# A two-layer graph network on one core: four small moves in a fixed instruction order (sums in the projection, byte casts in the attention, a fetch of rows, sums of the last product)

## The chip, the cores and the metric

The kernel runs on one core of one Trainium2 chip. The metric is the device time of one execution in microseconds (us). The kernel before was timed three times: 2682.81, 2682.03 and 2674.33 us, so its median is 2682.03 us. A profile of one more execution gives, for every instruction, when it ran and what it waited for.

## The reference, cut to what matters

```python
# x [3327, 512], adj [3327, 3327] (0 or 1, about 1% ones), W_stack [2, 512, 1024], weight [512, 512]; all float32
def gat(x, W, adj):
    Wh, Ws = split(x @ W, 2, axis=-1)
    a = softmax(Wh @ Ws.T, axis=-1) * adj
    return leaky_relu(a @ Wh + x, 0.01)

y = x
for l in range(2):
    y = gat(y, W_stack[l], adj)
x = layernorm(x + y)

bw = sign(weight)
ba = maximum(sign(x), 0)
out = relu(adj @ (ba @ bw.T))
return layernorm(x + out)
```

There are three kinds of large products: the projections and scores of each of the two attention layers, the attention's weighted sums `a @ Wh`, and at the end the aggregation `adj @ (...)` with a 0/1 matrix.

## The kernel before, in words

**Blocks and sums.** Rows are cut into 26 tiles of 128 (`P`). Two tiles are a pair (13 pairs, `NQ`), four tiles a chunk (7 chunks, `NC`). Nearly every large product is computed as a 2 x 2 block product with seven multiplications in place of eight. That needs sums of the left blocks (`left_sums`, L180 to L183) and of the right blocks (`right_sums`, L186 to L189) on VectorE, and copies (ScalarE) and additions (VectorE) that put the seven products together in PSUM and out of it (`seven`, L144 to L173; copies named p1, p5, u2, u3). In PSUM the lane `ch` has three banks, `acc` four, `tr` one.

**A fixed order.** No scheduler chooses the order of instructions. The Python code writes it out, and every engine (TensorE, VectorE, ScalarE, GpSimd as POOL, and SyncE, which only issues transfers) runs its own instructions strictly in the order in which they were written. Two helpers make the order. In the projection `weave` (L191) takes several lists of small steps and merges them, so that step i of a list of n lies at (i + 0.5)/n of the way. In the attention each step gathers pairs of a key and an action and runs them sorted by key (L911); a key of 0.6 means about 60% of the way through the step. Small blocks in SBUF come from one ring of 33 slots (`slot`), which are reused in order.

**The projection** (`project`, L243 to L449, once for each layer) computes for each chunk c, from the transposed rows `xT`:
- the "chains" `one` and `two` (`queries`): a product with the matrix `m`. They need the sums `xt` of the chunk (`sums`, four right sums made by `prepare(c)`), and give blocks `gsp`. At their end `done` (L400) stores three blocks, forms the four right sums of the results, and stores them also, all in `gs_d`.
- the "pairs" (`project_values(c, a)`, two for a chunk): first `keys` (L310), which makes the four left sums of the keys in tiles `s12` and `s34` and issues six stores to `xs_d` from POOL (L324 to L327), then seven products with the weights (L338), whose results stay in `wh`, and at the end `done` (L343), four right sums in tiles `t12` and `t34` with two stores to `ws_d`.
- the "turns": four transposes of the next chunk's rows (L263), and `prepare(c + 1)`.

The loop of L435 to L449 weaves these three lists for each chunk. The pairs of a chunk are created when its turn in the loop comes, so the first pair's `keys` opens the chunk, and both `done` steps close it.

**The attention** (`attention`, L463 to L933, once for each layer) runs 169 steps, 13 row halves g times 13 pairs q. The scores (L494) run 30 steps ahead of the values (L719). Between them lie, for one block of scores: the subtraction of the maximum (`shift`, L639, VectorE), the exponential (L642, ScalarE), a running sum (L650, VectorE), the mask by the adjacency block (`masked`, L655, VectorE), and four sums on POOL (L692 to L695, tile `as`). SyncE loads `ws`, `adj`, `xs` and, once for a chunk, `gs` (1792 KB).

**Byte blocks.** Since adj holds only 0 and 1, each block is also kept for the last product as seven small blocks in fp8, in a tile `ab` (tag `adj_b`, two buffers). `halved` (L658) casts three blocks on ScalarE (L663, L664). `halved_sums` (L666) makes four sums on VectorE (L674), `exact` (L679) checks on VectorE that the block is 0/1 (and takes adj's name out of the table), and `keep_blocks` (L676) issues the 112 KB store to `adj_d` from POOL. Each of the 169 blocks is kept once, about half of them in each layer. In the step's list the four have these keys, the last one in the following step:

```python
(-0.1, lambda: halved(*of)), (0.6, lambda: halved_sums(*of)),
(0.62, lambda: exact(*of)),
...
after.append((0.05, lambda of=of: keep_blocks(*of)))
```

**The end of a row half** (`finish`, L755 to L836) divides by the sum of the exponentials and adds the rows of x (`residual`), and in the second layer also takes the sign (`sign`, tile `ba`), transposes it (`turn`, tile `pbt`) and multiplies it by `bw` (`linear`). The rows come by `fetch(i)`: one load of 256 KB (`xres`) for the row tile in the first layer, two (`xres` and `x0`) in the second. `fetch(0)` is called twice in succession (L827, L828).

**The last product.** While the attention's last row half runs, `load_products` loads the rows `xw` and makes the right sums of the first 11 (`EARLY`) of 13 pairs (`product_sums`, in the tiles `wh`). After the last step the nine actions of the last `finish` run, with part of the last product between them (`fill`, L926). Then `finale` makes the product sums of the pairs 11 and 12 (L1074, L1075) and runs the rest of the aggregation (`aggregate`, L992).

Of the kernel before, what the change touches and what calls it, by code (L numbers as in the profile page):

```python
# [11 lines left out]
F8 = mybir.dt.float8e4  # L12
# [7 lines left out]
P = 128  # L20
# [9 lines left out]
def kernel(  # L30
# [15 lines left out]
    NQ = NT // 2  # L46
# [5 lines left out]
    def tiles_of(c):  # L52
        return range(c * CT, min(NT, (c + 1) * CT))
# [137 lines left out]
    def weave(*lists):  # L191

        at = [
            ((i + 0.5) / len(part), n, do)
            for n, part in enumerate(lists) for i, do in enumerate(part)
        ]
        for _, _, do in sorted(at, key=lambda e: e[:2]):
            do()
# [44 lines left out]
    def project(l, pre):  # L243
# [172 lines left out]
                for e in range(2):  # L416
                    nc.scalar.copy(m[:, 2 * e : 2 * e + 2], m_of[l][e])

        chains = {}

        def prepare(c):
            start, *chains[c] = queries(c, (ch_lane, ch_lane if c else acc_lane))
            if start:
                start()
# [10 lines left out]
        for c in range(NC):  # L435
            turns = []
            if c + 1 < NC:
                turns = [lambda k=k: transpose_x(c + 1, k, tr_lane) for k in range(KD)]
                turns.append(lambda: prepare(c + 1))
            if c + 2 < NC:  # L440
                load_x(c + 2)
            if c == 0:
                weave(*chains[c], turns)
            else:
                one, two = chains[c]
                pairs = []
                for a in range(len(tiles_of(c)) // 2):
                    pairs += project_values(c, a, acc_lane)
                weave(one + two, pairs, turns)  # L449

    bw = []

# [10 lines left out]
    def attention(l, att):  # L463
# [193 lines left out]

        def halved(g, q):  # L658

            at = adj[g, q]  # L660
            t = att.tile([P, 7, P], F8, tag="adj_b", bufs=2, name=f"ab_{g}_{q}")
            adj[g, q, "b"] = t
            nc.scalar.copy(t[:, 0:2], at[:, :, :P], saturate=False)  # L663
            nc.scalar.copy(t[:, 2], at[:, 1, P:], saturate=False)  # L664

        def halved_sums(g, q):  # L666
            at, t = adj[g, q], adj[g, q, "b"]
            a11, a21, a12, a22 = (at[:, k, ts(i, P)] for k in range(2) for i in range(2))
            s1, s2, s3, s4 = (t[:, i] for i in range(3, 7))
            for to, a, b, op in (  # L670
                (s1, a21, a22, ALU.add), (s2, s1, a11, ALU.subtract),
                (s3, a11, a21, ALU.subtract), (s4, a12, s2, ALU.subtract),
            ):
                nc.vector.tensor_tensor(to, a, b, op, saturate=False)  # L674

        def keep_blocks(g, q):  # L676
            nc.gpsimd.dma_start(out=adj_d[g][:, q], in_=adj.pop((g, q, "b")))

        def exact(g, q):  # L679

            at = adj.pop((g, q))
            i = g * NQ + q
            nc.vector.scalar_tensor_tensor(
                at, at, 0.0, at, ALU.is_gt, ALU.not_equal, accum_out=cnt[:, i : i + 1],
            )
# [69 lines left out]
        def finish(g):  # L755

            sm = total[g][:, 0]
            nc.gpsimd.tensor_tensor(sm, sm, total[g][:, 1], ALU.add)
            pz = ps_tr.tile([P, 2, P], F32, tag="tr", name=f"pz_{l}_{g}")
            rz = small.tile([P, 2], F32, tag="rz", name=f"rz_{l}_{g}")  # L760
            hs = out_.pop(g)
            mine = half_tiles(g)
            held = {}

            def norm():
                for i in range(2):
                    nc.tensor.transpose(pz[:, i], sm[:, ts(i, P)], ident)
                nc.vector.reduce_sum(rz, pz, axis=AX.X)
                nc.vector.reciprocal(rz, rz)

            def fetch(i):
                t = mine[i]
                span = slice(t * P, t * P + rows(t))
                for name, src in (("xres", x1_d), ("x0", x)) if last else (("xres", x),):
                    xr = ring.tile([P, D], F32, tag="xr", name=f"{name}_{l}_{t}")
                    load_rows(nc.sync, xr, src[span, :], rows(t))
                    held[i, name] = xr

            def residual(i):
                t, hh = mine[i], hs[i]  # L780
                r = rows(t)
                span = slice(t * P, t * P + r)
                nc.vector.scalar_tensor_tensor(
                    hh[:r], hh[:r], rz[:r, i : i + 1], held[i, "xres"][:r], ALU.mult, ALU.add
                )
                nc.vector.scalar_tensor_tensor(
                    hh[:r], hh[:r], NEG_SLOPE, hh[:r], ALU.mult, ALU.max
                )
                if last:
                    nc.vector.tensor_tensor(hh[:r], hh[:r], held[i, "x0"][:r], ALU.add)  # L790
                load_rows(nc.gpsimd, h_d[span, :] if last else x1_d[span, :], hh, r)

            def sign(i):

                t, hh = mine[i], hs[i]
                r = rows(t)
                st = small.tile([P, 6], F32, tag="bn", name=f"bn_{t}")
                nc.vector.bn_stats(st[:r], hh[:r])
                nc.vector.bn_aggr(mv[:r, t, :], st[:r])
                ba = held[i] = att.tile([P, D], BF16, tag="ba", bufs=1, name=f"ba_{t}")  # L800
                nc.vector.tensor_scalar(ba[:r], hh[:r], mv[:r, t, 0:1], None, ALU.is_gt)

            def turn(i):
                r = rows(mine[i])
                pt = ps_tr.tile([P, KD, P], BF16, tag="tr", name=f"pbt_{mine[i]}")
                for k in range(KD):
                    nc.tensor.transpose(pt[:, k, :r], held[i][:r, ts(k, P)], ident_h[:r, :r])
                held[i] = att.tile([P, KD, P], BF16, tag="baT", bufs=1, name=f"baT_{mine[i]}")
                nc.scalar.copy(held[i][:, :, :r], pt[:, :, :r])

            def linear(i):

                t = mine[i]
                r = rows(t)
                pw = ps_tr.tile([P, D], F32, tag="tr", name=f"pxw_{t}")
                for k in range(KD):
                    nc.tensor.matmul(
                        pw[:r], held[i][:, k, :r], bw[k], start=(k == 0), stop=(k == KD - 1)
                    )
                if g == NQ - 1:  # L820
                    nc.scalar.copy(xw[t][:r], pw[:r])
                    return
                xh = att.tile([P, D], F16, tag="ba", bufs=1, name=f"xwh_{t}")
                nc.scalar.copy(xh[:r], pw[:r])
                load_rows(nc.gpsimd, xw_d[t], xh, r)

            fetch(0)  # L827
            fetch(0)  # L828
            if not last:
                return [norm, lambda: residual(0), lambda: fetch(1), lambda: None,  # L830
                        lambda: residual(1)]
            return [
                norm, lambda: residual(0), lambda: (sign(0), fetch(1)), lambda: turn(0),
                lambda: linear(0), lambda: residual(1), lambda: sign(1), lambda: turn(1),
                lambda: linear(1),
            ]  # L836
# [3 lines left out]
        else:  # L840
# [17 lines left out]
            n = len(steps) - end - 2  # L858
# [15 lines left out]
        later, after = [], []  # L874
        for v in range(-LOOK - 4, len(steps)):
# [17 lines left out]
            if 0 <= v + 2 < len(steps):  # L893
                s2 = steps[v + 2]
                work += [(0.01, lambda: running(*s2)), (0.4, lambda: masked(*s2))]
                of = blocks.get(v + 2)
                if of:
                    work += [
                        (-0.1, lambda: halved(*of)), (0.6, lambda: halved_sums(*of)),
                        (0.62, lambda: exact(*of)),  # L900
                    ]
                    after.append((0.05, lambda of=of: keep_blocks(*of)))
            if later:
                work += [(0.7, later.pop(0))]
            if 0 <= u < len(ahead):
# [17 lines left out]
            (g, b, p, i) for g in range(2) for b in range(3) for p in range(EARLY)  # L923
            for i in BANKS[b]
        ]
        for n, do in zip((4, 16, 48, 8, 12, 12, 12, 8, 8), later):  # L926
            do()
            for e in fill[:n]:
                aggregate(*e)
            fill = fill[n:]  # L930
# [40 lines left out]
    def product_sums(p):  # L971
        x1, x2 = xw[2 * p], xw[2 * p + 1]
        xt[p] = wh[p].bitcast(F16).rearrange("p a n -> p (a n)")[:, : 4 * HD].rearrange(
            "p (i n) -> p i n", i=4
        )
        right_sums(x1[:, :HD], x1[:, HD:], x2[:, :HD], x2[:, HD:], *(xt[p][:, i] for i in range(4)))
# [20 lines left out]
    def finale(att):  # L997
# [73 lines left out]
            nc.vector.tensor_copy(flag_i, flag)  # L1071

        constants()
        for p in range(EARLY, NQ):  # L1074
            product_sums(p)  # L1075
        load_h(0)
        for g in range(NQ):
            todo = [
# [103 lines left out]
```

## Time and profile before

| What | Value |
|---|---|
| times of three runs | 2682.81, 2682.03, 2674.33 us (median 2682.03) |
| the profiled execution's own time | 2681.87 us |
| its span in the profile | 2680.1 us |
| granted TensorE clock, mean | 0.996 |
| TensorE matmuls, busy | 2622.6 us, 98% of the span |
| TensorE weight loads, busy (beside the matmuls) | 2273.6 us, 85% |
| VectorE, busy | 2059.8 us, 77% |
| ScalarE, busy | 813.0 us, 30% |
| POOL, busy | 1093.4 us, 41% |
| DMA | 648.84 MB, 242 GB/s in the mean |

The span reaches from the first to the last recorded instruction; the execution's own time lies 1.8 us above it. A line of a timeline or a group names the line of the code, the engine, the operation, and then the tile that is written and those that are read ("s<-xT"). "x4" is the number of instructions in succession that are put together. In square brackets stands the idle time of the engine just before the line, in us, and what ended it. A row of the waits has the waiting engine, tile and line, what it waited for, and then three numbers: the sum in us, how many times, and the longest. A row of the windows has the stretch, its length, the busy time (and number of instructions) of TensorE, its weight loads, VectorE, ScalarE and POOL, the granted clock, the share of the DMA engines and their GB/s.

### The profile page before, as it was taken

The page shows a single profiled execution, that of the slowest core. Times are in us where ns is not written, and L with a number is a line of the kernel's source. Part 1 is how long each engine was busy: PE and PEld are TensorE (multiplying, and loading weights), DVE is VectorE, ACT ScalarE, POOL GpSimd, SP SyncE. Part 2 cuts the span into 40 slices and gives each one's busy share as a digit, 9 for nine tenths or more (in the row PEclk, how much of TensorE's full clock was granted, in tenths as well). Part 3 has the DMA queues.
Part 4 walks back from the last instruction along what each step waited for, and adds up shares of the span by engine and source line. Part 5 has one row for each costly group of instructions (what it writes and reads, how often), then busy time and mean ns, then how long its engine had stood idle before and what let it go on. Part 6 is the DMA issues. An engine that isn't in the chain of part 4 may idle for free. (4 is left out here: it accounts for less than half of the span.)

```text
span 2680.1 us, 40370 instructions
## 1 busy us (share of the span) xinstructions
PE 2622.6 (98%) x12839; PEld 2273.6 (85%) x12864; DVE 2059.8 (77%) x4211; ACT 813.0 (30%) x2000; POOL 1093.4 (41%) x2029
## 2 busy tenths in 40 slices
PE   9999999999999999999999999999999999999897
PEld 7888888888888888887888888888888888888787
DVE  5554888899888996666755488988899888767876
ACT  3333332333323332221332333333333333222142
POOL 2450343444434444546543044444444444455510
PEclk9999999999999999999999999999999999999999
DMA  5754777777777776777865578777777777787874
GB/s 197 259 199 151 253 253 238 241 278 249 256 234 251 276 243 235 232 252 237 292 207 180 196 230 285 252 248 268 245 273 253 260 265 230 236 269 268 285 247 159
DMA packets 290800, 648.84 MB, mean 242 GB/s; under 512 B 32765, under 2 KB 147295, under 8 KB 289046
## 3 DMA queue, kind: packets, MB, share of 16 engines
q1 hardware_dynamic: 254822, 539.75, 60.8%
q0 software_dynamic: 35760, 106.45, 10.9%
q8 instruction: 105, 1.72, 0.2%
q14 instruction: 113, 0.93, 0.1%
HBM read 539.13 MB, written 106.93 MB: 241 GB/s over the span
## 5 line engine op out<-in xcount | busy, mean ns | idle before, releaser
L494 PE MATMUL pZ<-gs,xs 128*128 128x256 f32 x2496 | 640.3, 381 | 10.9 <-ACT u L511 9.7
L692 POOL TENSOR_TENSOR as<-s 128x128 f32<-128x128 f32 x338 | 163.9, 485 | 1011.1 <-DVE s L655 661.3
L494 PEld LDWEIGHTS pZ<-gs,xs 128*128 128x128 f32 x2496 | 475.1, 191 | 79.6 <-ACT u L511 12.8
L719 PE MATMUL acc<-ws,s 128*128 128x256 f32 x1352 | 403.1, 380 | 0.0
L719 PE MATMUL acc<-wh,s 128*128 128x256 f32 x1352 | 356.1, 380 | 0.0
L719 PE MATMUL acc<-ws,as 128*128 128x256 f32 x1352 | 349.9, 380 | 5.5 <-DMA ws<-ws_d 4.6
L494 PE MATMUL pY<-gs,xs 128*128 128x256 f32 x1248 | 320.3, 379 | 0.0
L642 ACT ACTIVATE s<-s 128x512 f32<-128x512 f32 x338 | 213.4, 631 | 317.3 <-DVE s L639 316.8
L719 PEld LDWEIGHTS acc<-ws,as 128*128 128x128 f32 x1352 | 254.8, 190 | 46.7 <-issue 5.1
L719 PEld LDWEIGHTS acc<-wh,s 128*128 128x128 f32 x1352 | 257.6, 191 | 35.4
L719 PEld LDWEIGHTS acc<-ws,s 128*128 128x128 f32 x1352 | 256.5, 190 | 34.5
L564 DVE TENSOR_TENSOR top<-top,s 128x512 f32<-128x512 f32 x312 | 222.8, 726 | 74.7 <-ACT s L551 49.3
L494 PEld LDWEIGHTS pY<-gs,xs 128*128 128x128 f32 x1248 | 237.0, 190 | 32.3
L639 DVE TENSOR_TENSOR s<-s,off 128x512 f32<-128x512 f32 x338 | 247.9, 734 | 0.1
L655 DVE TENSOR_TENSOR s<-s,adj 128x512 f32<-128x512 f32 x338 | 236.6, 700 | 10.6 <-DMA adj<-in_adjT_dram 1.7
L650 DVE TENSOR_TENSOR total<-total,s 128x512 f32<-128x512 f32 x312 | 231.1, 741 | 0.0
L511 ACT COPY u<-pZ 128x256 f32<-128x256 f32 x312 | 116.1, 372 | 328.8 <-PE pZ L494 328.2
L694 POOL TENSOR_TENSOR as<-s 128x128 f32<-128x128 f32 x338 | 205.1, 607 | 26.5
L536 DVE TENSOR_TENSOR s<-p,u 128x256 f32<-128x256 f32 x156 | 66.7, 428 | 184.0 <-ACT u L511 183.9
L719 PE MATMUL acc<-wh,as 128*128 128x256 f32 x676 | 203.4, 383 | 0.0
L693 POOL TENSOR_TENSOR s<-s 128x128 f32<-128x128 f32 x338 | 182.2, 539 | 27.7
L695 POOL TENSOR_TENSOR as<-s,as 128x128 f32<-128x128 f32 x338 | 179.4, 531 | 26.5
(206 smaller groups left out, 3910.0 us busy)
## 6 DMA issues: line engine op xcount, KB each, us to landing
ws<-ws_d SPq DMA_DIRECT2D x338, 512.0 KB, 3.8
xs<-xs_d SPq DMA_DIRECT2D x182, 512.0 KB, 5.9
adj<-in_adjT_dram SPq DMA_DIRECT2D x324, 256.0 KB, 4.4
xs<-xs_d SPq DMA_DIRECT2D x156, 384.0 KB, 6.4
gs_d<-gsp POOLq DMA_DIRECT2D x88, 256.0 KB, 2.9
gs<-gs_d SPq DMA_DIRECT2D x12, 1792.0 KB, 10.5
adj_d<-ab POOLq DMA_DIRECT2D x169, 112.0 KB, 3.9
ahl<-adj_d SPq DMA_DIRECT2D x78, 224.0 KB, 4.9
```

The lines of the kernel that those rows point to most:

```text
L494: nc.tensor.matmul(ch[bank], xs[c, q, a][:, k], gs[c][:, b, k], start=(start and k == 0), stop=(k == 1), skip_group_check=True,)
L511: nc.scalar.copy(ch[name], ch[bank])
L564: nc.vector.tensor_tensor(top[i], top[i], t, ALU.max)
L639: nc.vector.tensor_tensor(s, s, off[g].to_broadcast([P, 2, HW]), ALU.subtract)
L642: nc.scalar.activation(sc[g, q], sc[g, q], AF.Exp)
L650: nc.vector.tensor_tensor(total[g], total[g], sc[g, q], ALU.add)
L655: nc.vector.tensor_tensor(s, s, adj[g, q], ALU.mult)
L692: nc.gpsimd.tensor_tensor(s3, a11, a21, ALU.subtract)
L693: nc.gpsimd.tensor_tensor(a21, a21, a22, ALU.add)
L694: nc.gpsimd.tensor_tensor(s2, a21, a11, ALU.subtract)
L695: nc.gpsimd.tensor_tensor(s4, a12, s2, ALU.subtract)
L719: nc.tensor.matmul(acc[g][i // 2][:, i % 2], a[i], b[i], start=(q == 0 and i % 2 == 0), stop=(q == NQ - 1), skip_group_check=True,)
```

## The change

It has four parts, and it neither adds nor drops any computation.

- **Projection.** The first pair of chunk c + 1 is created while chunk c is written out. Its `keys` step goes into the turns of chunk c, before `prepare(c + 1)`. The `done` step of chain `two` and the `done` step of the last pair are taken from the end of their lists and put at the head of the turns of the next chunk (`rest`), or after the loop for the last.
- **Byte blocks.** The tile `ab` is allocated by `halved_sums` at key 0.6. The casts of `halved` come behind it at 0.61 (before: at -0.1), `exact` stays at 0.62, and the store of `keep_blocks` goes from 0.05 to 0.5 of the following step.
- **Rows.** `finish` calls `fetch(0)` once.
- **Product sums.** Those of pair 11 are made beside the action with number 6 of the last `finish`; `finale` makes those of pair 12 alone.

```diff
@@ project
-        chains = {}
+        chains, pairs_of, rest = {}, {}, []
...
             if c + 1 < NC:
                 turns = [lambda k=k: transpose_x(c + 1, k, tr_lane) for k in range(KD)]
-                turns.append(lambda: prepare(c + 1))
+                pairs_of[c + 1] = project_values(c + 1, 0, acc_lane)
+                turns += [pairs_of[c + 1].pop(0), lambda: prepare(c + 1)]
+            turns = rest + turns
+            rest = [chains[c][1].pop()] if chains[c][1] else []
             if c + 2 < NC:
                 load_x(c + 2)
             if c == 0:
                 weave(*chains[c], turns)
             else:
                 one, two = chains[c]
-                pairs = []
-                for a in range(len(tiles_of(c)) // 2):
+                pairs = pairs_of[c]
+                for a in range(1, len(tiles_of(c)) // 2):
                     pairs += project_values(c, a, acc_lane)
+                rest.append(pairs.pop())
                 weave(one + two, pairs, turns)
+        for do in rest:
+            do()
@@ attention
         def halved(g, q):
-            at = adj[g, q]
-            t = att.tile([P, 7, P], F8, tag="adj_b", bufs=2, name=f"ab_{g}_{q}")
-            adj[g, q, "b"] = t
+            at, t = adj[g, q], adj[g, q, "b"]
             nc.scalar.copy(t[:, 0:2], at[:, :, :P], saturate=False)
             nc.scalar.copy(t[:, 2], at[:, 1, P:], saturate=False)
 
         def halved_sums(g, q):
-            at, t = adj[g, q], adj[g, q, "b"]
+            at = adj[g, q]
+            t = adj[g, q, "b"] = att.tile(
+                [P, 7, P], F8, tag="adj_b", bufs=2, name=f"ab_{l}_{g}_{q}"
+            )
...
-            fetch(0)
             fetch(0)
...
-                        (-0.1, lambda: halved(*of)), (0.6, lambda: halved_sums(*of)),
-                        (0.62, lambda: exact(*of)),
+                        (0.6, lambda: halved_sums(*of)), (0.62, lambda: exact(*of)),
+                        (0.61, lambda: halved(*of)),
                     ]
-                    after.append((0.05, lambda of=of: keep_blocks(*of)))
+                    after.append((0.5, lambda of=of: keep_blocks(*of)))
...
-        for n, do in zip((4, 16, 48, 8, 12, 12, 12, 8, 8), later):
+        for e, (n, do) in enumerate(zip((4, 16, 48, 8, 12, 12, 12, 8, 8), later)):
             do()
+            if e == 6:
+                product_sums(EARLY)
             for e in fill[:n]:
                 aggregate(*e)
             fill = fill[n:]
@@ finale
-        for p in range(EARLY, NQ):
-            product_sums(p)
+        product_sums(NQ - 1)
```

## The prediction

> **What bounds the kernel now.** I read the page first (busy time by engine), then the waits of TensorE, the timeline around its idle stretches, and the waits of the engines and queues behind them. The times are 2682.81, 2682.03 and 2674.33 us; the profiled execution took 2681.87 us with a span of 2680.1 us, 0.16 us from the median of 2682.03, so I make the sum against 2681.87.
>
> ```profile
> PE 2622.6 (98%) x12839; PEld 2273.6 (85%) x12864; DVE 2059.8 (77%) x4211; ACT 813.0 (30%) x2000; POOL 1093.4 (41%) x2029
> ```
>
> TensorE is the bound: 2680.1 - 2622.6 = 57.5 us idle, of which some 15 us lie behind its last matmul (the chain of waits has its last piece end at 2665.3 us). The change neither adds nor drops a matmul, so it can only win back some of the remaining 42 us, or make new gaps. The waits of TensorE (us in total, times, longest):
>
> ```profile
> PE pZ_wh L338 <- DVE s L181: 12.3, 9, 1.7
> PE pZ L494 <- ACT u L511: 9.7, 5, 4.3
> PE acc L719 <- DMA ws<-ws_d: 4.6, 3, 3.7
> PE agg L992 <- DVE wh L187: 2.0, 2, 1.5
> PE pZ L494 <- ACT p L511: 1.2, 2, 0.7
> ```
>
> Each of these rows is one target of the change. The first is the projection: at a chunk's beginning the keys' sums of the first pair (L180 to L183, tile s) stand on VectorE behind two other blocks.
>
> ```profile
> 81.36 0.68 DVE L186 TENSOR_TENSOR gsp<-b,gsp 128x512 f32<-128x512 f32 x1
> ...
> 83.89 0.42 DVE L186 TENSOR_TENSOR t<-wb,wh 128x256 f32<-128x256 f32 x1
> ...
> 85.35 0.42 DVE L180 TENSOR_TENSOR s<-xT 128x256 f32<-128x256 f32 x1
> 85.81 0.42 DVE L181 TENSOR_TENSOR s<-s,xT 128x256 f32<-128x256 f32 x1
> 86.38 1.10 PE L338 MATMUL pZ_wh<-wsum,s 128*128 128x256 f32 x4 [1.45 <-DVE s L181]
> ```
>
> The second row comes from ScalarE: before the byte cast it waits for a store that frees the byte tile ab (two buffers), and everything behind it on ScalarE is late, the copies u and p that TensorE needs included.
>
> ```profile
> ACT ab L663 <- DMA adj_d<-ab: 29.9, 10, 7.2
> ```
>
> (SyncE's queue, further down, waits as long for the second fetch of the same rows:)
>
> ```profile
> SPq L115 <- DMA xres<-x_d: 58.6, 14, 6.7
> ```
>
> ```profile
> 407.05 0.54 POOL L677 DMA_DIRECT2D adj_d<-ab  x1
> 411.21 0.56 POOL L677 DMA_DIRECT2D adj_d<-ab  x1
> ...
> 418.20 0.40 ACT L663 CAST ab<-adj 128x256 fp8e4<-128x256 f32 x1 [7.22 <-DMA adj_d<-ab]
> 419.12 2.08 PE L494 MATMUL pZ<-gs,xs 128*128 128x256 f32 x4 [4.29 <-ACT u L511]
> ```
>
> A wait of 7.2 us on ScalarE costs TensorE 4.3; another of 6.6 costs 3.7; four of 3.0 to 3.7 cost 0.5 to 0.7 each; those under 0.8 cost nothing. ScalarE thus hides about 2.9 us.
>
> **What the Trainium skill says.** "Perfetto Trace Analysis", Identifying the Most-Contended Engine: matmul busy share misleads, LDWEIGHTS busy share is better; here 85%, and the same verdict. "TensorE: Matmul & The Clock Gate", Step-by-step: matmuls stay in program order, only weight loads are pulled ahead. The trace agrees: in the 1.45 us gap no later product ran. "DMA: Bandwidth & Descriptors", Anatomy of one DMA: a transfer's semaphore wait is spent on the issuing sequencer, before dispatch (SyncE's 58.6 us agree), and a transfer costs about 2.0 us plus bytes/436e9. That would be 2.3 us for the 112 KB store; the trace has 2.0 at least, 3.9 in the median, 11.1 at most, and I use those.
>
> **Part A, projection order.** The edit moves the four keys' sums and six stores of a chunk's first pair to about 0.81 of the chunk before, ahead of the x sums at 0.94, and pushes the results' sums (4 x 0.69 us of gsp with seven stores, 4 x 0.42 of t with two) into the next chunk, at 0.06 and 0.19. Eight chunks have the gap, 1.44 to 1.66 us: 12.0 of the 12.3 (the ninth, 0.36, lies ahead of layer 1's first chunk and is not touched). What is late next? A chunk takes 27.6 us. The x sums (4 x 0.68) end about 1.0 us into the new chunk and are needed at 2.5/14 of it, 4.9 us. The gsp sums then end at 3.8, and the adds that empty the products' banks at 4.6; those banks are asked for again past the chunk's middle. VectorE has 17 us of work in 27.6. POOL issues the same 23 transfers (some 14 us), and the six stores read a tile that is complete by 0.72. So nothing new is on TensorE's path: **-12.0** (a third of the gaps left: -8; all nine gone: -12.3).
>
> **Part B, byte casts behind the sums.** Nothing is added: 169 x (0.41 + 0.30) us on ScalarE, the 169 x 4 sums on VectorE and 169 stores are the same. But the tile's first writer is now VectorE, at 0.60 of a step of about 6 us, the cast follows at 0.61, not -0.1, and the store goes from 0.05 to 0.5 of the next step, so POOL issues it behind that step's four sums (2.2 us). Take the tight case:
>
> ```profile
> 493.12 0.54 POOL L677 DMA_DIRECT2D adj_d<-ab  x1
> ...
> 496.29 0.46 POOL L695 TENSOR_TENSOR as<-s,as 128x128 f32<-128x128 f32 x1
> ...
> 497.79 0.41 ACT L663 CAST ab<-adj 128x256 fp8e4<-128x256 f32 x1 [0.66 <-DMA adj_d<-ab]
> ...
> 500.68 0.50 DVE L674 TENSOR_TENSOR ab<-adj 128x128 fp8e4<-128x128 f32 x1
> ```
>
> Before, the store had from 493.12 to 497.1 = 4.0 us before ScalarE stopped. After, it is issued at 496.75 and VectorE asks at 500.68: 3.9 us. The wait is not removed; **it changes engine**. Behind the waiting sum stand the check of the block, the next shift and, on ScalarE, the next exponential. That exponential can be late by about 2.3 us where the next copy is u2 and 3.9 where it is c21, both read off the timeline from exponential to copy to the matmul that reuses the bank. For the two big cases, both with a 1.8 MB gs load in flight: issued at 411.1 instead of 407.05, the store lands near 418.7, as the neighbour of 411.21 did (7.5 us); VectorE would be there at 415.0, waits 3.7 us, and TensorE loses 0 to 1.4. The four cases of 3 us: stores issued at the new times took 4.4 to 5.4 us against 3.9 of room, 0.5 to 1.5 us of wait, nothing lost. I leave 2 us for the two large ones and for new tight cases, of 10.9 now: **-8.9** (best -10.9; worst, all of it comes back on VectorE, 0; a further loss is the rival below). The check (L683) now also waits for the cast: where the cast follows u2 it ends some 0.5 us after VectorE's four sums do; VectorE was ahead there and idles for u (L536, 184 us in all), so I cost it at nothing.
>
> **Part C, one fetch.** In finish, fetch(0) ran twice. 13 transfers go in layer 0 and 26 in layer 1, 39 x 256 KB = 10 MB of 649, and with them SyncE's 58.6 us of waiting. It pays only where ws is late, in the last row:
>
> ```profile
> 2478.00:2530.00 52.00, 44.09 (x202) 35.49 (x203) 48.67 (x95) 8.90 (x16) 37.01 (x68) 1.00 0.85 296
> ```
>
> There VectorE is busy 48.67 of 52 us and its one long wait is 1.18 us for adj, at 2492.55, behind the same blocked queue. With ws in time, TensorE would run into VectorE's masks instead, so of the 4.6 us only VectorE's 1.18 is won: **-1.2** (0 to -4.6).
>
> **Part D, finale.** One of two blocks of product sums moves ahead to a place where VectorE waits. The remaining block starts where the first did, 0.93 us earlier (its L187 ran at 2551.19, the first block's at 2550.26): **-0.9** (0 to -2.0).
>
> Sum: 12.0 + 8.9 + 1.2 + 0.9 = 23.0; 2681.87 - 23.0 = **2658.9 us**, 0.86% less.
>
> **Rivals.** (1) The ab wait passes whole to TensorE by way of VectorE: B is 0 to -2, the rest holds, 2666 to 2669. For it: store room is no larger (3.9 against 4.0 us), and the exponential hangs on VectorE. Against: the large cases shrink, since the store is issued later under the same load.
> (2) VectorE fills up. In the stretch of 850 to 900 us it is busy 47.17 of 50. Some 40 tight blocks, each costing TensorE 0.3 us, are +12 in place of B's -8.9, with A, C and D at -14: about 2680, no change that can be told. Against: the waits fall mostly where VectorE is ahead.
> (3) Slower: the slot ring. The gs_d stores now come after a chunk's start, while chain two's first copy and the keys' sums, at 0.53 to 0.54 of that chunk, take slots that these stores free. They land, by the median 2.9 us, near 10 us and are asked for at 14.7. If they landed after some 17 us, TensorE would stand still in each of ten chunks; from 3 us each (+30 against B, C and D's -11 and A's old 12 gone) the kernel gets slower, 2690. The longest gs_d store took 7.6 us, so it is unlikely.
>
> **The numbers.** Forecast 0.74, rival (1) 0.14, (2) 0.07, (3) 0.05. A measurement of this kernel can tell about 0.3% (8 us) from no change. Faster 0.88 = 0.74 + 0.14; same 0.07; slower 0.05. Range: all best ends give 12.3 + 10.9 + 4.6 + 2.0 = 29.8, so 2652, and 2650 for the scatter of the runs; the other end takes in rival (1) with A a little short, 2670.
>
> **What would show it.** Right: no wait of pZ_wh for s beyond 0.4 us; u and p waits of TensorE down to about 2 us; a new row of VectorE waiting for the adj_d store, 10 to 30 us; SyncE's wait for xres gone, the wait for ws near zero, but waits on as or ba in the last row; the agg wait about half. Wrong: new TensorE waits on copies h or on s in the projection, or on as or u through the attention.

## The result, and the profile after

The changed kernel took 2653.22 us (median of four runs, 2652.55 to 2654.84); the kernel before beside it 2682.06 us. The ratio is 0.9900 with a 95% interval of 0.9881 to 0.9918. That is 28.8 us less, where 23.0 were forecast: the direction and the range hold, and the forecast time of 2658.9 us is 5.7 us too high. The profiled execution took 2652.55 us with a span of 2650.7 us, so from trace to trace the gain is 29.4 us.

The first line of the page after, busy time by engine:

```profile
PE 2614.6 (99%) x12839; PEld 2271.0 (86%) x12864; DVE 2046.3 (77%) x4211; ACT 812.1 (31%) x2000; POOL 1091.3 (41%) x2029
```

TensorE's idle time in the span fell from 57.5 to 36.1 us, 21.4 us. But its *busy* time fell as well, by 8.0 us, with the same number of matmuls. No step of the forecast has that term; it is the first sign that the recorded gaps are not the whole price of a stall.

TensorE's waits after (us in total, times, longest):

```profile
PE pxt L263 <- DMA xr<-in_x_dram: 5.6, 3, 3.7
PE pbt L814 <- DVE ba L808: 4.1, 2, 2.9
PE ptop L602 <- DVE top L594: 2.6, 4, 0.8
PE pY L500 <- ACT p L517: 2.2, 4, 1.1
PE pZ L500 <- ACT u L517: 1.7, 2, 1.0
PE agg L1000 <- DVE wh L187: 1.3, 1, 1.3
PE acc L726 <- POOL as L701: 1.2, 2, 0.8
...
PE pZ_wh L338 <- DVE s L181: 0.4, 1, 0.4
...
PE acc L726 <- DMA ws<-ws_d: 0.2, 1, 0.2
```

The reader is to see that the row for s is down to the one wait that was not touched (9 waits and 12.3 us before), that ws is down to 0.2 us (4.6 before) and ba has grown (1.6 before), and that p and u are 3.9 us together (10.9 before).

To see where the time came from, I took the start of the same instruction in both traces (the first score product of a layer, the transposes of the row halves, the last matmuls) and the difference between the two:

| Stage | gain in us | forecast |
|---|---|---|
| projection, layer 0 | 7.3 | 6.0 (A) |
| attention, layer 0 | 9.1 | B, see below |
| projection, layer 1 | 7.3 | 6.0 (A) |
| attention, layer 1, up to the last row half | 2.1 | B; both layers 8.9 |
| last row half | 0.5 | 1.2 (C) |
| last product, up to the last matmul | 1.3 | 0.9 (D) |
| behind the last matmul | 1.9 | 0 |
| sum, before rounding | 29.4 | 23.0 |

### The profile page after: what moved, and what is told of

It is laid out like the page before. It is cut to its first block, busy times and chain, and to the rows that moved or that the text cites. A ratio compares the mean times of both kernels' runs of the same rounds, so it can differ in the third digit from the quotient of the medians.

```text
span 2650.7 us, 40451 instructions
## 1 busy us (share of the span) xinstructions
PE 2614.6 (99%) x12839; PEld 2271.0 (86%) x12864; DVE 2046.3 (77%) x4211; ACT 812.1 (31%) x2000; POOL 1091.3 (41%) x2029
## 6 DMA issues: line engine op xcount, KB each, us to landing
gs<-gs_d SPq DMA_DIRECT2D x12, 1792.0 KB, 10.9
```

## What a stall of TensorE costs besides its gap

Two things lie in the table that the forecast's sum of gaps left out.

**The refill.** In the trace before, the four matmuls ahead of the gap of 1.45 us start at 83.91 us, the four behind it at 86.38, the next four at 87.31. The timeline of TensorE after, at the same place of the code (start, us of the group):

```profile
83.11 1.03 PE L338 MATMUL pZ_wh<-wsum,s 128*128 128x256 f32 x4
83.98 1.03 PE L394 MATMUL pZ_g<-xt,msum 128*128 128x256 f32 x4
84.84 1.03 PE L338 MATMUL pY_wh<-wsum,s 128*128 128x256 f32 x4
```

The groups follow each other every 0.865 us, though each is shown as 1.03 us long: the shown length reaches past the start of the next matmul. A gap in the records is counted from that late end. Before, the group came 2.47 us after the one ahead, so the stall cost 2.47 - 0.865 = 1.61 us, and the next came 0.93 instead of 0.865 after that: 1.67 us lost behind a recorded 1.45.

**The clock.** The windows around the first large stall in the trace before (busy of TensorE, weight loads, VectorE, ScalarE, POOL; then the granted clock, the DMA share and GB/s); the matmul behind the gap starts at 419.12:

```profile
416.00:418.00 2.00, 0.00 (x0) 0.00 (x0) 0.00 (x0) 0.00 (x0) 0.00 (x0) 1.00 0.87 356
418.00:420.00 2.00, 0.88 (x2) 0.79 (x3) 0.83 (x2) 1.40 (x4) 0.00 (x0) 0.50 0.46 168
420.00:422.00 2.00, 2.00 (x6) 1.56 (x6) 1.97 (x6) 0.37 (x1) 1.48 (x3) 0.50 0.00 0
422.00:424.00 2.00, 2.00 (x7) 1.56 (x6) 1.97 (x5) 0.00 (x0) 1.01 (x2) 0.50 0.09 36
424.00:426.00 2.00, 2.00 (x9) 1.70 (x8) 1.97 (x4) 0.90 (x2) 0.00 (x0) 0.80 0.98 288
426.00:428.00 2.00, 2.00 (x11) 1.77 (x10) 1.59 (x4) 0.00 (x0) 1.47 (x3) 1.00 0.99 329
```

Here TensorE counts as busy without a break, but does 6, 7 and 9 matmuls in 2 us instead of 11, at a clock of 0.50. Added up, 3.40 us of clock are missing from 418 to 426 us, and 3.42 from 742 to 750 at the second large stall. Some 0.9 of these 6.8 us fall into the ends of the two gaps, where no matmul runs; the other 5.9 make matmuls slower. The changed kernel at the same wait for the same store:

```profile
406.00:408.00 2.00, 2.00 (x11) 1.75 (x10) 1.01 (x3) 0.00 (x0) 1.01 (x3) 1.00 1.01 429
408.00:410.00 2.00, 2.00 (x11) 1.76 (x10) 0.00 (x0) 0.00 (x0) 1.36 (x3) 1.00 0.97 402
410.00:412.00 2.00, 2.00 (x11) 1.77 (x10) 0.83 (x4) 0.82 (x4) 0.00 (x0) 1.00 1.05 389
```

VectorE and ScalarE stand still (0.00 from 408 to 410), as before, but TensorE has its 11 matmuls in each window. The only place after where the clock falls before the end is in the last row half, behind the gap of 2.93 us for ba, with 1.70 us missing:

```profile
2484.00:2486.00 2.00, 0.11 (x2) 0.11 (x3) 1.87 (x5) 0.00 (x0) 1.26 (x3) 0.89 0.58 206
2486.00:2488.00 2.00, 2.00 (x8) 1.73 (x8) 1.97 (x6) 0.13 (x1) 0.65 (x3) 0.50 0.00 0
2488.00:2490.00 2.00, 2.00 (x8) 1.63 (x8) 1.87 (x5) 0.97 (x2) 0.56 (x2) 0.76 0.38 57
```

The Trainium skill, "TensorE: Matmul & The Clock Gate", What's actually happening, says that a monitor halves TensorE's clock after an idle window of about 3.4 us (3413 ns) and frees it after a busy one, and that the windows run freely. These traces agree on the portion: 1.70 us missing is 3.4 us at half clock. I had read this page for the order of matmuls, and the clock row of the profile's page shows 9 in all 40 slices, so I did not apply it to the stalls.

## The experiments

All times are medians; the kernel before ran beside them, with 2682.21, 2682.51 and 2681.60 us in the three groups.

**1. Each part alone on the kernel before.** The edits are the four parts of the diff above.

Part A alone:

> The kernel before with part A alone. Theory 1 (the forecast's own sum: a stall of TensorE costs its recorded gap): eight gaps of 1.44 to 1.66 us go, -12.0 us. Theory 2 (a stall costs its gap plus a refill: in the kernel before the group of four matmuls behind the gap of 1.45 us starts 2.47 us after the last one, where 0.865 us is the rhythm, so 1.6 us are lost, and with the slower group behind it 1.7): 8 x 1.7 = -13.6 to -14.0 us. Rival (the slot ring gives something back): less than -10 us and waits on copies in the projection. The five waits of pZ for u (9.7 us) stay.

Measured: 2665.35 us, ratio 0.9937 (0.9923 to 0.9950), 16.9 us less (13.4 to 20.7). Its trace, of the fastest of the five executions, is 20.0 us shorter: the two projections give 7.5 and 6.0 us, 13.6 together before rounding; 5.7 lie in the attention, which this part does not touch; the end behind the last matmul is 2.1 us shorter; and the last product is 1.3 us longer. In the attention the two large stalls lost 1.70 us of clock each, where they lost 3.4 each in the trace before. So theory 2 holds for the projection itself, and the slot ring gave nothing back.

Part B alone:

> The kernel before with part B alone. Theory 1 (gaps only): the gaps of TensorE behind ScalarE fall from 10.9 us to the 5 us or so that the changed kernel shows (waits for u 1.7, p 2.2 and some of ptop), so -5 to -9 us. Theory 2 (a gap of about 4 us also halves the granted clock for some 6 us afterwards, which costs another 3 us each, and there are two of them): -11 to -12 us, and the clock at 1.00 in the stretches where the kernel before has 0.97. Rival (the wait comes back whole by way of VectorE): 0 to -2 us.

Measured: 2674.73 us, ratio 0.9969 (0.9958 to 0.9980), 7.5 us less. This is where theory 1 puts it, and less than theory 2. The trace shows why: the two large stalls are gone, but gaps of 1.99 us (for p, at 477.7) and 2.19 us (for u, at 1884.8) are there in their place, and each costs a portion of 1.70 us of clock. (The profiled execution was the slowest of the seven, 2678.33 us; what the others lost isn't known.) Theory 2 is right on the price and took too little account of what would come late next.

Parts C and D alone:

> The kernel before with part C alone. Forecast: -1.2 us, the wait for ws near zero in the last row. Rival 1 (all of the wait is won): -4.6 us. Rival 2 (VectorE, full in the last row, gives it back as waits for ba and as, and a gap of 3 us there may halve the clock): 0 to +2 us.

> The kernel before with part D alone. Forecast: -0.9 us, one wait of agg for wh of about 1.5 us less the 0.9 us that the other block takes, the rest unchanged. Rival (the sums put ahead delay the last sign or turn): 0 or slower. A part of the 1.9 us by which the end behind the last matmul is shorter in the changed kernel would show here if it belonged to this part.

C: 2677.87 us, ratio 0.9984 (0.9978 to 0.9991), 4.3 us less (2.4 to 5.9). D: 2679.59 us, ratio 0.9989 (0.9981 to 0.9998), 2.6 us less (0.5 to 5.1). In D's trace, from the last value product to the last matmul, the gain is 0.95 us, which is the forecast; as a whole this trace is only 0.3 us shorter, so it does not show where the rest of the 2.6 us lies. C's trace is 6.3 us shorter. The last row half gives 1.0 us, with a new gap of 2.92 us for ba and 1.70 us of clock lost behind it; 1.4 us lie in the second layer's attention ahead of it, 1.6 us in the first layer's, where one of the large stalls lost a portion of clock less, and 2.1 us behind the last matmul.

The four alone add up to 31.3 us, together they give 28.8. One thing is counted twice in the sum: the end behind the last matmul is 2.1 us shorter in the traces of A alone and of C alone, and 1.9 us shorter, once, in that of the changed kernel.

**2. Parts C and D undone in the changed kernel.**

> The changed kernel with the second fetch of the same rows put back (part C undone). If part C was worth what the forecast says: +1.2 us. If it was worth what it gave alone on the kernel before: +4 us, with the waits for ws (or for adj behind the same queue) back in the last row. If VectorE gives it all back in the last row: 0, or less than 0 by the slow clock behind the gap of 2.9 us for ba (1.7 us).

```diff
             fetch(0)
+            fetch(0)
             if not last:
```

Measured: 2655.67 us, ratio to before 0.9901 (0.9885 to 0.9918), by the medians 2.5 us more than the changed kernel; the two intervals overlap. The last row half shows an exchange of waits. TensorE's list now has

```profile
PE acc L726 <- POOL adj L625: 3.5, 1, 3.5
```

with ba down to 1.0 us from 4.1: either the blocked queue or VectorE holds TensorE there, and that stage changes by only 0.2 us, with 3.4 us of clock missing in it, where the changed kernel has 1.7. So VectorE does give C back in the last row half. Of the 3.8 us by which this trace is longer, 2.3 lie in the two attentions ahead of the last row half. By the medians C is worth 2.5 us here and 4.3 us alone, more than the 1.2 I gave it, and in part not where I put it; which of the attention's waits make it up these runs don't settle.

> The changed kernel with both blocks of product sums in the finale (part D undone). Forecast: +0.9 us (the block's own time on VectorE, 0.93 us), wait of agg for wh two times and 2.0 us in place of 1.3. With a slow clock behind the longer wait: +2.6 us (0.9 and a portion of 1.7). Rival: 0.

```diff
-            if e == 6:
-                product_sums(EARLY)
...
-        product_sums(NQ - 1)
+        for p in range(EARLY, NQ):
+            product_sums(p)
```

Measured: 2654.31 us (ratio to before 0.9899, 0.9883 to 0.9916), 1.1 us more than the changed kernel. The two intervals overlap; it is the trace that shows the part, with 0.94 us in the last product. Part D is as forecast.

**3. Which of part B's two edits brings the gain?** One moves the casts behind the sums, the other moves the store from 0.05 to 0.5 of the following step.

> The kernel before, only the store of ab at 0.5 of the following step and not at 0.05; the casts stay ahead of the step at -0.1. If the gain of part B were in the store's new place: as part B, -7 us. If the place of the cast is what counts (behind the copies that TensorE needs): the store comes some 3 us later and ScalarE asks for the tile as early as before, so its wait grows from 30 us, and the kernel is slower, +10 to +60 us: many of the 167 blocks would then wait up to 2 us longer than ScalarE can hide.

```diff
-                    after.append((0.05, lambda of=of: keep_blocks(*of)))
+                    after.append((0.5, lambda of=of: keep_blocks(*of)))
```

Measured: 2785.16 us, ratio 1.0382 (1.0363 to 1.0400), 102.7 us slower. I expected 10 to 60. Rows of its waits:

```profile
ACT ab L663 <- DMA adj_d<-ab: 226.5, 74, 8.9
...
PE pZ L494 <- ACT p L511: 47.7, 16, 6.0
...
PE pZ L494 <- ACT u L511: 29.7, 14, 3.8
```

That is 77 us of TensorE's gaps for p and u, and behind 15 places a lower clock, 1.70 to 5.12 us missing at each.

> The kernel before, only the casts behind the sums at 0.61 with the tile taken at 0.6; the store stays at 0.05 of the following step. The store then has some 6 us before the tile is asked for again, not 3.9. If the cast's place is what counts: at least as good as part B alone, -7 to -14 us, and the wait for the store nearly gone on both engines. If the store at 0.05 is harmful in itself (POOL issues it ahead of the four sums that the values need): less than part B.

```diff
-                        (-0.1, lambda: halved(*of)), (0.6, lambda: halved_sums(*of)),
-                        (0.62, lambda: exact(*of)),
+                        (0.6, lambda: halved_sums(*of)), (0.62, lambda: exact(*of)),
+                        (0.61, lambda: halved(*of)),
...
# with the tile allocated in halved_sums, as in the change
```

Measured: 2667.89 us, ratio 0.9944 (0.9931 to 0.9958), 14.6 us less: twice part B. On the kernel before, the late store takes back half of what the casts' new place brings. The waits for ab here, and then those of the changed kernel:

```profile
ACT ab L661 <- DMA adj_d<-ab: 12.0, 2, 6.1
DVE ab L675 <- DMA adj_d<-ab: 9.5, 2, 4.8
```

```profile
ACT ab L667 <- DMA adj_d<-ab: 25.8, 16, 5.4
DVE ab L681 <- DMA adj_d<-ab: 21.5, 13, 4.1
```

With the store early, two long waits are left on each engine, those beside the 1.8 MB loads. My expectation that these too would be nearly gone is wrong. The timeline of the first:

```profile
406.19 0.44 SPq L476 DMA_DIRECT2D gs<-gs_d  x1
406.91 0.54 POOL L678 DMA_DIRECT2D adj_d<-ab  x1
...
418.65 0.29 DVE L675 TENSOR_TENSOR ab<-adj 128x128 fp8e4<-128x128 f32 x1 [4.68 <-DMA adj_d<-ab]
418.70 0.41 ACT L661 CAST ab<-adj 128x256 fp8e4<-128x256 f32 x1 [5.94 <-DMA adj_d<-ab]
```

The store of 406.91 goes out behind the large load and frees the tile 11.7 us later. ScalarE waits 5.94 us, nearly the 7.2 of before, and TensorE has no gap over 0.3 us there except 0.5 us at the next ptop. The wait is not shorter so much as it is in a harmless place: behind the copies that TensorE asks for, not ahead of them.

**4. A third byte tile.** There is room for it in layer 0 only.

> The kernel before, with three buffers for ab in layer 0 (two in layer 1, where there is no room for a third) and nothing else. If the wait of the cast for the store of ab is the cause of the two large stalls: the waits for u of 4.3 and 3.7 us go, and with them the slow clock behind them (two times 3.4 us in the profile of before), -10 to -15 us, and the clock does not fall in the stretches around 420 and 745 us. If something else holds ScalarE there (the scores' own order): 0 to -2 us.

> The changed kernel, with three buffers for ab in layer 0. If what is left of the wait (VectorE 4.1 us and ScalarE 5.4 us at most) still costs TensorE: the waits for p (2.2 us) and part of ptop go, -2 to -4 us. If these come from the new order of VectorE itself: 0.

```diff
-tag="adj_b", bufs=2
+tag="adj_b", bufs=3 - l
```

On the kernel before: 2668.90 us, ratio 0.9951 (0.9937 to 0.9964), 13.6 us less. Both large stalls are gone, and no clock is missing before the last product. So the wait for the store was their cause. On the changed kernel: 2648.43 us, ratio 0.9873 (0.9856 to 0.9891), 4.8 us less than without; no wait for p is left, and in layer 0's attention no gap over 0.3 us but the ones at the first and last ptop and poff.

**5. Stalls on purpose.** Is it the gap that lowers the clock, or the large load that is in flight there?

> The changed kernel with 5 to 24 extra copies of u2 on ScalarE (about 0.37 us each) at 40 places, four pairs in each of five chunks and in both layers, so that TensorE is held for different lengths. The computation is the same. Theory (a stall of TensorE costs its gap and then whole portions of about 1.7 us of half clock): behind each gap the clock loses 0, 1.7 or 3.4 us and nothing between; nothing behind gaps well under 2 us, always something above 4 us. Rival (the slow clock in the kernel before belongs to the large gs load that is in flight there, not to the gap): the clock stays at 1.00 behind gaps that have no such load beside them.

```diff
                 copied("u2", "Z")
+                if 1 <= c <= 5 and q % 3 == 1 and q < NQ - 1:
+                    for _ in range(5 + (7 * (c - 1) * 4 + 7 * (q // 3) + 3 * l) % 20):
+                        nc.scalar.copy(ch["u2"], ch["Z"])
```

One run: 2888.13 us. Every gap of TensorE over 0.4 us in its trace, without the start (where no matmul had yet run for long), sorted by length, with the clock missing behind it:

| gap | number | 0 missing | 1.7 us | 3.4 us | 5.1 us |
|---|---|---|---|---|---|
| under 2.0 us | 22 | 22 | 0 | 0 | 0 |
| 2.0 to 2.93 us | 7 | 2 | 5 | 0 | 0 |
| 3.2 to 8.1 us | 26 | 0 | 8 | 15 | 3 |

Three of them, from the timeline (the gap in brackets), and then windows behind or, with the last gap, inside and behind them:

```profile
2061.84 1.13 PE L500 MATMUL pZ<-gs,xs 128*128 128x256 f32 x4 [1.94 <-ACT u L534]
...
957.79 1.65 PE L500 MATMUL pZ<-gs,xs 128*128 128x256 f32 x3 [2.41 <-ACT u L534]
...
774.19 2.08 PE L500 MATMUL pZ<-gs,xs 128*128 128x256 f32 x4 [7.26 <-ACT u L534]
```

```profile
2062.00:2064.00 2.00, 2.00 (x10) 1.77 (x11) 0.52 (x2) 1.54 (x5) 0.54 (x1) 1.00 0.99 388
...
958.00:960.00 2.00, 2.00 (x5) 1.65 (x6) 1.73 (x4) 0.61 (x4) 0.00 (x0) 0.50 0.54 197
960.00:962.00 2.00, 2.00 (x8) 1.63 (x8) 1.21 (x3) 1.30 (x4) 0.45 (x1) 0.71 0.00 0
...
770.00:772.00 2.00, 0.00 (x0) 0.00 (x0) 0.00 (x0) 1.84 (x6) 0.00 (x0) 0.50 0.58 211
...
778.00:780.00 2.00, 2.00 (x6) 1.56 (x6) 0.28 (x1) 0.00 (x0) 1.76 (x4) 0.50 0.04 8
```

The clock is lost in whole portions of 1.7 us, behind 31 gaps that are spread over both attentions, while the kernel has only 12 of the large loads; it is lost also where the DMA engines move only 0 to 211 GB/s, and not behind the gap of 1.94 us with 388 GB/s beside it. The rival with the load falls.

The length of a gap does not decide alone. In other traces gaps of 3.70 us (before), 3.34 (part A alone), 3.24 (three byte tiles on the kernel before) and three of 3.02 to 3.53 (late store) lost nothing, and in three traces (parts A and B alone, three byte tiles on the kernel before) the two gaps of 1.5 and 0.5 us that open the finale lost 1.70 us.

What sorts all of them is a fixed grid in time. Any two changes of the clock in one trace lie a whole number of steps of 3.413 us apart: in the trace before it falls at 417.98 and 742.25 us and rises at 424.81 and 749.08, and from 424.81 to 742.25 are 317.44 us, 93 steps. With each of the 14 traces cut into cells of its own grid (from 30 us on, up to the last matmul), the clock falls at the end of all 65 full-speed cells in which TensorE is idle for 1.96 us or more, and of no other; the idlest of the others has 1.94 us. Of the cells at half clock, it rises at the end of all 65 with 0.54 us or less idle, and of none of the 36 with 0.61 or more. Some cells, from the kernel before, from part B alone and from part A alone:

```profile
2486.46:2489.88 3.42, 1.64 (x8) 1.11 (x6) 3.35 (x5) 0.00 (x0) 3.19 (x6) 1.00 0.82 271
2489.88:2493.29 3.41, 1.49 (x7) 1.36 (x8) 2.23 (x4) 0.63 (x1) 1.48 (x4) 1.00 0.91 289
```

```profile
475.42:478.83 3.41, 1.43 (x7) 1.04 (x6) 1.98 (x7) 1.15 (x4) 1.01 (x2) 1.00 0.88 337
478.83:482.24 3.41, 3.41 (x9) 2.71 (x9) 2.96 (x6) 0.63 (x1) 1.24 (x3) 0.50 0.29 78
```

```profile
405.68:409.10 3.42, 1.61 (x8) 1.08 (x6) 0.00 (x0) 0.00 (x0) 0.00 (x0) 1.00 0.97 408
409.10:412.51 3.41, 1.45 (x7) 1.29 (x8) 1.40 (x4) 1.63 (x5) 0.22 (x1) 1.00 0.65 253
412.51:415.92 3.41, 3.41 (x10) 2.70 (x9) 3.34 (x8) 0.52 (x2) 2.28 (x5) 0.50 0.40 118
```

The gap of 3.70 us lies across two cells in each of which TensorE is busy for 1.49 us or more, and costs no clock. The gap of 1.99 us lies in one cell and costs one cell at half clock, which is 1.7 us. The gap of 3.77 us at the first large stall of part A alone leaves one of its two cells busy enough. Where the grid lies against the kernel differs between executions: the same gap starts at 414.83 us in the trace before and at 414.96 in that of part D alone, whose code is the same up to there, and the clock falls 3.15 and 2.42 us into it. So the price of a gap differs as well, and with it the time: of the 53 timings of the kernel before beside the experiments, the one with the highest mean clock, 0.998, took 2674.24 us, and the 15 with 0.994 took 2683.8 us in the mean.

**6. The better version.**

> The changed kernel with the store of ab back at 0.05 of the following step and three buffers for ab in layer 0. If the store's late place is what held part B down: the waits of TensorE for u and p in layer 1 (1.7 us, two) go too, and ptop's beyond those that stay in every kernel; against the changed kernel -5 to -7 us, 2646 to 2648 us. If POOL's early issue costs something: the same as with three buffers alone, 2648 us, or more.

```diff
-                [P, 7, P], F8, tag="adj_b", bufs=2, name=f"ab_{l}_{g}_{q}"
+                [P, 7, P], F8, tag="adj_b", bufs=3 - l, name=f"ab_{l}_{g}_{q}"
...
-                    after.append((0.5, lambda of=of: keep_blocks(*of)))
+                    after.append((0.05, lambda of=of: keep_blocks(*of)))
```

Measured: 2646.42 us (2646.35 to 2647.62), ratio to before 0.9870 (0.9853 to 0.9886), 6.8 us less than the changed kernel and 2.0 us less than with three buffers alone (single timings of these last two overlap). No engine waits for the store any more, and

```profile
PE pZ L500 <- ACT u L517: 1.3, 2, 0.7
```

is all that TensorE still waits for ScalarE in the attention. It is the fastest of all versions here.

## Why the prediction was right, and where it was off

- **Bound.** Right: what went from TensorE's idle time, 21.4 us, is the larger part of the gain. The other 8.0 us are in its busy time, for which the sum had no term. (In the trace before, the last matmul ends at 2666.7 us, so 13.4 us lay behind it, not some 15, and 44 us were to be won.)
- **A, forecast -12.0, in the trace -14.6.** The mechanism held in every point: no wait for s over 0.4 us, no new wait, and POOL and the slot ring (rival 3) gave nothing back. The term that was mis-sized is the price of one stall, which I took as its recorded gap of 1.45 us; it cost 1.67 us. Eight times the difference is 1.8 of the 2.6 us; the other 0.8 us I can't assign. Its two moves, the keys' sums ahead and the results' sums behind, were not tried apart.
- **B, forecast -8.9, in the trace of all four parts -11.2 in the two attentions.** By experiment 2, 2.3 us of that hang on part C, which leaves about 8.9 for B; alone it gave 7.5. That the number is met is luck, two errors against each other. The 10.9 us of recorded gaps behind ScalarE did not fall to 2 but to some 4.6 us (p 2.2, u 1.7, ptop 0.7 more than before). And 6.8 us of missing clock at the two large gaps, 5.9 of them with matmuls running, were not in my sum at all. "The wait changes engine" was half right: VectorE's new row has 21.5 us, within the 10 to 30 that I named, but ScalarE's own 29.9 us stayed at 25.8, as both now wait for the same store. My step for the four cases of 3 us, "nothing lost", failed: with the store late there are 16 waits instead of 10, and p and u pay for them. Experiment 3 shows the cause, the store at 0.5, which I had priced only by the room it leaves (3.9 against 4.0 us).
- **C, forecast -1.2.** The last row half went as described: ws near zero, waits on ba and as in its place, VectorE full. The trace gives 0.5 us there; without the 1.7 us of clock behind the wait for ba it would be about 2. By the medians C is worth 2.5 and 4.3 us, and the traces of experiments 1 and 2 have 1.4 and 2.3 us of gain in attention steps ahead of the last row half, where I had priced SyncE's 58.6 us of waiting at nothing. So the step "it pays only where ws is late, in the last row" is wrong as far as single traces tell.
- **D, forecast -0.9.** Right: 0.94 and 0.95 us where it is taken away or put in alone. The wait for wh fell from 2.0 to 1.3 us, not by half.
- **The end behind the last matmul**, 1.9 us shorter, was in no step. The time from VectorE's last instruction to the end is 7.8 us before and 5.9 after, 5.8 to 6.3 us in all eight versions that have part A or part C, and 7.6 to 7.8 in the six that have neither. Neither part has an instruction there; by what way they set it stays open.
- **The other rivals.** Neither the wait coming back whole by way of VectorE (1) nor VectorE filling up (2) happened. That rival 1's tight room is real shows in experiment 3, where the same store, with the casts left at -0.1, makes the kernel 102.7 us slower.

## What to carry to other kernels

Price a stall of TensorE by the starts of its matmuls on both sides, not by the recorded gap, and look at the granted clock in windows of 2 us behind it: here a gap of 1.45 us cost 0.2 us extra, gaps over 3 us nearly always 1.7 to 5.1 us of clock, and no single gap under 1.9 us any. So the few long gaps are worth more than their sum, and it pays to break them up or to let the waiting instruction stand behind the copies that TensorE needs. When a change makes two moves for one purpose, price each one alone: here one of them brought 14.6 us, and the other took half of it back.

## What I had not expected of the hardware

- Gaps of 2.08 to 2.93 us are enough to halve TensorE's clock, in five of seven cases. The Trainium skill's page on TensorE's clock gate (the same section) speaks of an idle window of about 3.4 us; the traces agree on the length of the window, 3.413 us, and on its running freely, but 1.96 us idle within one was enough, and the measurement decides. Whether a gap of 2 to 3 us pays depends on how the grid cuts it.
- The lost clock is 1.70, 3.4 or 5.12 us, and nothing between, and a part of it can fall into the gap itself: behind the gap of 7.26 us the clock had already fallen before the first matmul came.
- A 112 KB store issued 0.7 us behind a 1.8 MB load freed its tile after 11.1 us in the kernel before (407.05 to 418.20) and 11.7 us in the version with the casts late, where its median is 3.9.
